# Layer 0 of a four-layer recurrent model: sums over eight neighbours, three additions and a state's four summands are written differently

## The chip, the cores and the metric

The kernel runs on one core of a Trainium2 chip. The metric is the device time of one execution in microseconds. Three runs of the kernel before took 3638.57, 3640.07 and 3646.86 us; the median is 3640.07. A separate, profiled execution took 3631.03 us.

Each core has five engines with queues of their own: TensorE (PE in the profile, its weight loads PEld), VectorE (DVE), ScalarE (ACT), GpSimd (POOL), and SyncE (SP), which here only starts DMA transfers. An engine works through its queue in order; engines wait for each other by semaphores.

## The reference, cut to what matters

The model has four layers; each computes `x + s * silu(g)` from a recurrent or attention branch s and an expert branch g. Only layer 0 is touched. Its branch s is a linear recurrence over time for 16 heads of 8 features, for 8 sequences of 512 tokens of 128 features:

```python
def step(S, inp):
    r_, w_, k_, v_, kk_, b_ = inp
    sab = jnp.einsum('bhvk,bhk->bhv', S, kk_)
    S = S * jnp.exp(w_)[:, :, None, :] + sab[..., None] * b_[:, :, None, :] + v_[..., None] * k_[:, :, None, :]
    y = jnp.einsum('bhvk,bhk->bhv', S, r_)
    return (S, y)
_, y = jax.lax.scan(step, S0, (rh, wh, kh, vh, kkh, bh))
mu = y.mean(-1, keepdims=True)
var = ((y - mu) ** 2).mean(-1, keepdims=True)
yn = (y - mu) / jnp.sqrt(var + 0.00064) * ln_w + ln_b
bonus = (r4 * k4 * time_faaaa).sum(-1, keepdims=True) * v4
out = (yn + bonus).reshape(B, T, C) * g
return out @ output.T
```

The vectors r, w, k, v, kk and b of every token come from the token and the one before it, through a difference xx (previous minus current), small matrix products and activations; kk is divided by its norm over the 8 features of a head. The expert branch picks tokens for each of 48 experts, runs a two-layer network on them and adds the results into an array in DRAM.

## The kernel before, in words

**Stages.** The 512 tokens are cut into four *stages* of 128 (`jt`, `JT` = 4). For each stage there are four pieces of work:

- *Front* (`front`, two halves of four sequences each, `hf`): features on the partitions. xx on Vector (L375), products on TensorE (L377 to L415), activations on ACT, the rest on Vector: L388 (four inputs), L443 and L444 (the sum of squares over 8 features, nrm), L449 to L454, and L455 (yb plus t1), L457, L459. The last writes Kt.
- *Back* (`back`): six arrays are transposed by TensorE (L619) and copied by ACT (L620) so that the 128 pairs of sequence and head lie on the partitions; then Vector prepares pairs of steps: bonus, dk, dr (L628 to L648), each a product and a reduce over 8, with a scratch tile `sg` of one buffer.
- *Scan* (L687 to L720): two tokens are treated in one step, so a stage has 64 steps, in eight *blocks* of eight (`SH` = 8). A block first prepares Z (L687, L691); a step then has five pairs of Vector instructions, one for each half of a state's rows: L700, L704, L706, L710, L712. Z holds for a step four summands of 8 x 8 elements; L710 and L712 add them in two rounds to the new state Hs. After the steps the block multiplies the states by r (L714, L715, L718) into HR and sums over 8 (L720) into Y.
- *Closing* (L721 to L764): a correction of Y (L723), mean and variance over 8 (L727 to L730), scale and offset on ACT (L736), addition of the bonus term (L739), eight transposes on TensorE (L748), the product with the gate (L749), transposes (L754) and the output product (L758).

**Experts.** `experts()` is a generator with 49 *turns*. A turn has one expert's first products (L562), for every second one the gathering of two more experts' tokens (L548, L552), and the former expert's second products (L574), transpose (L582), scaling and scatter (L585). Two turns are taken before each block, so all are done at the start of stage 3.

**What sets the order.** From here on TensorE's order is the order of the program text (`manual_schedule`): for each stage, the front and back of the *next* stage, then the experts' turns with what stands between them, then the closing of this stage. The queues of Vector, ACT and GpSimd are ordered by the framework's scheduler, ahead of time; the order is fixed when the kernel runs. The first stage's front stands earlier, beside the picking of tokens (L493 to L497), which is Vector work.

**Buffers.** `k.pa` is a ring of five PSUM banks for everything but the experts, which have three others. HR and Z have one buffer, Hs two, Y one.

## Time and profile before

| What | Value |
|---|---|
| Median of three runs | 3640.07 us |
| Profiled execution | 3631.03 us |
| Span of its instructions | 3629.3 us |
| Busy over the span: TensorE / Vector / ACT / GpSimd | 2764.3 / 2336.2 / 1642.4 / 745.4 us |
| Mean granted TensorE clock | 0.835 of full speed |
| First scan step (L700), last (L712) | 201.9 us, 856.1 us |
| Scan groups L700, L704, L706, L710, L712 (512 each), busy | 108.8, 87.6, 91.5, 91.6, 82.1 us |
| L720 (32), busy | 38.8 us |

The profile gives, for each group of instructions, the line, engine and operation, the output and input tiles with their shapes, how many there are, their busy time and the mean length of one in ns, and the idle time of the engine before them with what ended it. Busy time counts overlapping instructions once; Vector's short instructions overlap with the one before by some 0.08 us, so that mean lengths add up to more than the busy time. A timeline line has start, length, engine, line, operation and tiles, the count, and in brackets the idle time before it. A product of two 32-bit matrices shows as two records and two weight loads, a transpose as one. A window's line has its length, then busy time and count of each engine, the granted TensorE clock, the DMA share and GB/s.

### The profile page before, as it was taken

How to read it: one execution, taken by the hardware profiler on the slowest of the kernel's cores; microseconds unless marked ns; L12 is line 12 of the kernel's file. 1: busy time of each engine (PE TensorE's matmuls, PEld its weight loads, DVE VectorE, ACT ScalarE, POOL GpSimd, SP SyncE). 2: the span in 40 equal slices, each digit the busy share in tenths (PEclk: the TensorE clock that was granted, in tenths of full speed). 3: DMA queues.
4: the chain of work that ended last, by engine and by line, in shares of the span. 5: the costliest groups of instructions: out<-in, count | busy, mean ns of one | idle time of the engine just before them, and what ended most of it. 6: DMA issues, size and time to landing. Idle time of an engine off the chain costs nothing.

```text
span 3629.3 us, 44988 instructions
## 1 busy us (share of the span) xinstructions
PE 2764.3 (76%) x16390; PEld 1479.4 (41%) x16390; DVE 2336.2 (64%) x6346; ACT 1642.4 (45%) x3207; POOL 745.4 (21%) x845
## 2 busy tenths in 40 slices
PE   6164656512998898799999999998678877778777
PEld 4143444401444454344444444444334444444444
DVE  7989898998583234334445445445478787777776
ACT  5163545512544455233333333333266666655655
POOL 0004050400125553201101101101112222222121
PEclk8585757555789899799899899899878898878989
DMA  4003030311002222100000000000000000000000
GB/s 120 2 2 72 1 81 1 72 49 34 1 2 47 39 42 29 56 1 1 1 1 1 1 1 1 1 1 1 6 15 1 4 4 4 1 3 4 1 4 7
DMA packets 67519, 64.53 MB, mean 18 GB/s; under 512 B 5344, under 2 KB 59616, under 8 KB 66784
## 3 DMA queue, kind: packets, MB, share of 16 engines
q1 hardware_dynamic: 39264, 42.75, 3.8%
q0 software_dynamic: 19712, 14.69, 3.1%
q10 hardware_dynamic: 8320, 4.19, 0.4%
q8 instruction: 129, 2.11, 0.2%
q14 instruction: 94, 0.77, 0.1%
HBM read 43.80 MB, written 17.83 MB: 17 GB/s over the span
## 4 chain that ended last, share of the span: by engine, by line
PE 35%; DVE 16%; ACT 7%; issue 2%; POOL 2%; DMA 0%; POOLq 0%; ACTq 0%; DVEq 0%; SPq 0%
PE pa L1372 6%; PE pu L1390 6%; DVE nm L1972 4%; ACT at L1973 3%; PE pu L1969 3%; PE pf L1954 2%; DVE mpad L1404 2%; PE pf L1435 2%; PE pa L1486 1%; PE pa L1485 1%; ACT at L1422 1%; PE pa L1878 1%; PE pa L1509 1%; PE pa L1359 1%; PE pa L1515 1%
## 5 line engine op out<-in xcount | busy, mean ns | idle before, releaser
L1973 ACT ACTIVATE at<-pu,nm 128x512 f32<-128x512 f32 x512 | 347.9, 688 | 174.3 <-DVE nm L1972 154.5
L1972 DVE TENSOR_REDUCE nm<-pu 128x1 f32<-128x512 f32 x512 | 327.4, 683 | 75.4 <-PE pu L1969 74.8
L199 POOL TENSOR_SCALAR_AFFINE_SELECT at<-at 128x512 f32<-128x512 f32 x184 | 123.6, 672 | 1000.2 <-ACT at L1422 851.7
L1404 DVE TENSOR_REDUCE mpad<-pu 128x2 f32<-128x256 f32 (+3 forms) x256 | 199.2, 819 | 168.1 <-PE pu L1401 168.1
L1422 ACT ACTIVATE at<-pu 128x1024 f32<-128x1024 f32 (+3 forms) x256 | 171.8, 702 | 283.5 <-PE pu L1390 283.2
L1078 ACT ACTIVATE at<-pu,rsqrt 128x1024 f32<-128x1024 f32 (+3 forms) x256 | 191.1, 793 | 191.0 <-PE pu L1073 161.2
L1372 PE MATMUL pa<-hid,f 128*128 128x512 f32 x512 | 222.7, 593 | 0.0
L1969 PE MATMUL pu<-qT,kT 32*128 32x512 f32 x1024 | 203.1, 731 | 2.4 <-ACT at L1973 2.3
L1390 PE MATMUL pu<-qT,kT 32*128 32x512 f32 (+3 forms) x1024 | 160.6, 514 | 56.4 <-DVE mpad L1404 41.8
L748 PE MATMUL pa<-ident,Y 128*128 128x128 f32 x32 | 7.9, 425 | 211.2 <-DVE Y L739 211.2
L1954 PE MATMUL pf<-at,va 128*32 128x512 f32 x1024 | 163.1, 715 | 0.4 <-POOL va L1947 0.4
L1390 PE MATMUL pu<-kT,qT 32*128 32x128 f32 (+3 forms) x1024 | 150.8, 565 | 14.7 <-ACT at L1422 10.5
L548 POOL DMA_INDIRECT xg<-xn_d,idx x48 | 55.1, 1147 | 499.5 <-PE pf L552 318.5
L1372 PEld LDWEIGHTS pa<-hid,f 128*128 128x128 f32 x512 | 96.6, 190 | 119.5 <-issue 118.9
L1493 DVE SCALAR_TENSOR_TENSOR X<-X,u 128x512 f32<-128x512 f32 x56 | 38.7, 691 | 156.7 <-ACT u L1488 156.7
L1073 PE MATMUL pu<-qT,kT 32*128 32x512 f32 (+3 forms) x1024 | 130.3, 513 | 4.9 <-ACT at L1078 3.9
L1016 POOL DMA_INDIRECT f_d<-ys,idx x64 | 105.0, 1640 | 140.0 <-DMA f_d<-ys,idx 85.2
L1947 POOL TENSOR_TENSOR va<-V,sm 128x32 f32<-128x32 f32 x128 | 36.7, 286 | 463.6 <-DVE sm L1946 384.0
L1390 PEld LDWEIGHTS pu<-qT,kT 32*128 32x128 f32 x1024 | 67.3, 196 | 154.4 <-DVE mpad L1404 114.3
L1373 ACT ACTIVATE hid<-pa,f 128x512 f32<-128x512 f32 x64 | 44.0, 688 | 172.5 <-PE pa L1372 172.5
L1083 DVE TENSOR_TENSOR at<-at,ceiling 128x512 f32<-128x512 f32 x72 | 50.0, 695 | 102.3 <-ACT at L1078 91.4
L700 DVE TENSOR_TENSOR Z<-Hs,KE 128x96 f32<-128x96 f32 x510 | 108.8, 253 | 0.9
(610 smaller groups left out, 6682.8 us busy)
## 6 DMA issues: line engine op xcount, KB each, us to landing
w<-in_w_dram SPq DMA_DIRECT2D x24, 512.0 KB, 3.7
f_d<-zeros ACTq DMA_DIRECT2D x8, 512.0 KB
xn_d<-xn SPq DMA_DIRECT2D x8, 512.0 KB, 5.0
w<-in_w_dram SPq DMA_DIRECT2D x16, 256.0 KB, 3.2
w<-in_w_dram SPq DMA_DIRECT2D x24, 128.0 KB
f<-in_f_dram SPq DMA_DIRECT2D x1, 2888.0 KB, 11.9
xn<-in_x_dram SPq DMA_DIRECT2D x4, 512.0 KB, 9.0
Gt<-in_x_dram SPq DMA_DIRECT2D x4, 512.0 KB
```

The costliest lines, as they stand in the source:

```text
L199: self.nc.gpsimd.affine_select(a, a if src is None else src, pattern, ALU.is_ge, 0.0, base=0, channel_multiplier=-1)
L700: nc.vector.tensor_tensor(z[:, 0:3, v, :], bc(prev[:, v, :], 1, 3), bc(KE[:, o + t, 0:3, :], 2, 4), ALU.mult)
L1073: nc.tensor.matmul(pu[:, n, 0:m], q["kT"][r, g // 2, kc * P : kc * P + P], q["qT"][r, g, kc * P :], start=True, stop=True,)
L1078: nc.scalar.activation(at_[:, i : i + 2, 0:m], pu[:, :, 0:m], AF.Square, bias=k.rsqrt2, scale=32.0**-0.5)
L1372: nc.tensor.matmul(ps, fn[n][:, c0 : c0 + P], src[:, i, :], start=(i == 0), stop=(i == 3))
L1390: self.k.nc.tensor.matmul(pu[:, n, 0:m], a[r, c0 : c0 + P], b[r, q0 : q0 + m], start=True, stop=stop)
L1404: nc.vector.tensor_reduce(top[:, i : i + 2, 16], pu[:, :, 0:m], AX.X, ALU.max)
L1422: nc.scalar.activation(at_[:, i : i + 2, 0:m], pu[:, :, 0:m], AF.Exp, scale=8.0**-0.5)
L1954: nc.tensor.matmul(po[i * 32 : i * 32 + 32, :], va[:, kc, c0 : c0 + 32], E[:, i, :], start=(kc == 0), stop=(kc == JT - 1))
L1969: nc.tensor.matmul(pu, q["kT"][r, kc * P : (kc + 1) * P], q["qT"][r, g, :], start=True, stop=True)
L1972: nc.vector.tensor_reduce(nm[:, w], pu, AX.X, ALU.max, negate=True)
L1973: nc.scalar.activation(E[:, n, :], pu, AF.Exp, bias=nm[:, w], accum_out=sm[:, w])
```

## The change

- A helper `eighths` sums over groups of eight neighbours by TensorE: eight products with the identity as the stationary matrix, each with every eighth element as the moving one, accumulate in one PSUM bank. It takes the place of Vector's reduces L443, L630, L638, L640, L720, L727 and L730. Some results are read by Vector or ACT where they lie; bonus, dr and Y are copied to SBUF by ACT.
- Y's sums (`outputs`) are issued one block later, between the two expert turns that stand before the next block; the last block's come after the loop. HR gets two buffers.
- The difference xx is two products, with the identity and with its negative, and a copy by ACT; yb plus t1 is two products; the addition of the bonus term L739 goes into the transposes, which become pairs of products (L772 of the changed kernel).
- In the scan, L710 and L712 become one TENSOR_REDUCE for each half (L735 of the changed kernel), which adds the four summands of a state; its innermost axis has a step of 64 elements.

```diff
--- before.py
+++ after.py
@@ -357,6 +357,16 @@
         flat = lambda a: a.rearrange("p a b -> p (a b)")
         hv = lambda a: a.rearrange("p b (h n) -> p (b h) n", n=8)
         s_v = s.rearrange("p (b j) c -> p b j c", j=JT)
+        minus = cp.tile([P, P], F32, name="minus0")
+        nc.gpsimd.tensor_scalar(minus, k.ident, -1.0, None, ALU.mult)
+
+        def eighths(src):
+
+            ps = k.pa(src.shape[:2])
+            for i in range(8):
+                nc.tensor.matmul(ps, k.ident, src[:, :, i], start=(i == 0), stop=(i == 7))
+            return ps
+
 
         own = cp.tile([P, 4, C], F32, name="own0")
         for i, n in enumerate(("receptance", "key_w", "key_w", "value")):
@@ -371,8 +381,11 @@
                 bs = slice(hf * 4, hf * 4 + 4)
                 cur, prev = xT[:, bs, t0 + 1 : t0 + P + 1], xT[:, bs, t0 : t0 + P]
                 ht = lambda nm, sh=(P, 4, C): hp.tile(list(sh), F32, name=nm)
-                xx = ht("xx")
-                nc.vector.tensor_tensor(xx, prev, cur, ALU.subtract)
+                xx = k.pa((P, 4, C))
+                nc.tensor.matmul(xx, k.ident, prev, start=True, stop=False)
+                nc.tensor.matmul(xx, minus, cur, start=False, stop=True)
+                xs = ht("xx")
+                nc.scalar.copy(xs, xx)
                 ps = k.pa((P, 4, C))
                 nc.tensor.matmul(ps, w1m, cur, start=True, stop=False)
                 nc.tensor.matmul(ps, w1p, prev, start=False, stop=True)
@@ -385,7 +398,7 @@
                     q = slice(f * 32, f * 32 + 32)
                     nc.tensor.matmul(ps, cn["maa_w2"][q, :], mix[q, :, :], start=True, stop=True)
                     t.append(ht(f"xf{f}"))
-                    nc.vector.scalar_tensor_tensor(t[f], ps, cn["maa"][:, f : f + 1], xx, ALU.add, ALU.mult)
+                    nc.vector.scalar_tensor_tensor(t[f], ps, cn["maa"][:, f : f + 1], xs, ALU.add, ALU.mult)
                 trg, twa, tk_, tv_ = t
 
                 def both(ps, w, t):
@@ -440,8 +453,7 @@
                 pn = tokens((cur, own[:, 2]), (tk_, own[:, 2]), (lk, cn["k_w2"][:, 0:C]))
                 nc.scalar.activation(t2, pn, AF.Square)
                 nrm = ht("nrm", (P, 64))
-                nc.vector.tensor_reduce(nrm, hv(t2), AX.X, ALU.add)
-                nc.vector.tensor_scalar(nrm, nrm, 1e-24, None, ALU.max)
+                nc.vector.tensor_scalar(nrm, eighths(hv(t2)), 1e-24, None, ALU.max)
                 nc.scalar.activation(t1, t1, AF.Exp, scale=-1.0)
                 nc.scalar.activation(t1, t1, AF.Ln, bias=1.0)
                 nc.scalar.activation(nrm, nrm, AF.Ln)
@@ -452,9 +464,11 @@
                 nc.vector.scalar_tensor_tensor(a_, a_, 1.0, not_ma, ALU.subtract, ALU.mult)
                 pk = tokens((cur, own[:, 1]), (tk_, own[:, 1]))
                 nc.vector.scalar_tensor_tensor(a_, a_, 1.0, pk, ALU.add, ALU.mult)
-                nc.vector.tensor_tensor(yb, yb, t1, ALU.add)
-                nc.scalar.activation(F["EWt"][:, bs, :], yb, AF.Exp, scale=-1.0, bias=k.less_half)
-                nc.vector.scalar_tensor_tensor(yb, yb, 0.5, mk_, ALU.add, ALU.mult)
+                ps = k.pa((P, 4, C))
+                nc.tensor.matmul(ps, k.ident, yb, start=True, stop=False)
+                nc.tensor.matmul(ps, k.ident, t1, start=False, stop=True)
+                nc.scalar.activation(F["EWt"][:, bs, :], ps, AF.Exp, scale=-1.0, bias=k.less_half)
+                nc.vector.scalar_tensor_tensor(yb, ps, 0.5, mk_, ALU.add, ALU.mult)
                 nc.scalar.activation(t1, yb, AF.Exp, scale=-1.0)
                 nc.vector.tensor_tensor(F["Kt"][:, bs, :], a_, t1, ALU.mult)
 
@@ -627,18 +641,21 @@
             bonus = bp.tile([P, P], F32, name="bonus", bufs=2)
             tt(t, Rs.rearrange("p t s n -> p (t s) n"), BK[:, 1].rearrange("p t s n -> p (t s) n"), ALU.mult)
             tt(t, t, bc(cn["time_faaaa"], 1, P), ALU.mult)
-            nc.vector.tensor_reduce(bonus, t, AX.X, ALU.add)
-            t = work().rearrange("p (a t n) -> p a t n", a=2, n=8)
-            dk = bp.tile([P, 2, HT], F32, name="dk")
+            nc.scalar.copy(bonus, eighths(t))
+            pairs = lambda: work().rearrange("p (a t n) -> p a t n", a=2, n=8)
+            both = lambda t: eighths(t.rearrange("p a t n -> p (a t) n"))
             dr = bp.tile([P, 2, HT], F32, name="dr", bufs=2)
             bk = BK[:, :, :, 0, :]
             kk, kk2, w, w2 = (KE[:, :, i, :] for i in range(4))
             b2, r = BK[:, 0, :, 1, :], Rs[:, :, 0, :]
+            t = pairs()
             tt(t, bk, bc(kk2, 1, 2), ALU.mult)
-            nc.vector.tensor_reduce(dk, t, AX.X, ALU.add)
+            dk = both(t).rearrange("p (a t) -> p a t", a=2)
+            t = pairs()
             tt(t, bk, bc(r, 1, 2), ALU.mult)
-            nc.vector.tensor_reduce(dr, t, AX.X, ALU.add)
+            nc.scalar.copy(dr.rearrange("p a t -> p (a t)"), both(t))
             tt(bk, bk, bc(w2, 1, 2), ALU.mult)
+            t = pairs()
             tt(t, bc(dk, 3, 8), bc(b2, 1, 2), ALU.mult)
             tt(bk, bk, t, ALU.add)
             tt(r, r, w, ALU.mult)
@@ -656,12 +673,18 @@
         carry = cp.tile([P, 8, 8], F32, name="carry0")
         nc.gpsimd.memset(carry, 0.0)
         ready = back(*first)
+
+        def outputs(HR, y):
+
+            nc.scalar.copy(y, eighths(HR.rearrange("p t s v n -> p (t s v) n")))
+
         for jt in range(JT):
             G, KE, BK, Vs, Rs, bonus, kr = ready
             if jt + 1 < JT:
                 ready = back(*front(jt + 1))
             Y = bp.tile([P, P, 8], F32, name="Y")
             yp = Y.rearrange("p (t s) v -> p t s v", s=2)
+            last = None
             for o in range(0, HT, SH):
                 if jt == JT - 1 and o // SH >= HT // SH - JT:
 
@@ -679,8 +702,10 @@
                         nc.vector.tensor_tensor(s_v[:, :, j, :], f, old, ALU.add)
                     else:
                         held = f, old
-                for _ in range(2):
-                    next(side, None)
+                next(side, None)
+                if last:
+                    outputs(*last)
+                next(side, None)
 
                 Z = up.tile([P, SH, 4, 8, 8], F32, name="Z", bufs=1)
                 for i in range(2):
@@ -707,28 +732,27 @@
                             z[:, 0:2, v, :], bc(sab[:, h], 3, 8), bc(BK[:, 0, o + t], 2, 4), ALU.mult
                         )
                     for h, v in halves:
-                        nc.vector.tensor_tensor(z[:, 0:2, v, :], z[:, 0:2, v, :], z[:, 2:4, v, :], ALU.add)
-                    for h, v in halves:
-                        nc.vector.tensor_tensor(Hs[:, t, v, :], z[:, 0, v, :], z[:, 1, v, :], ALU.add)
-                HR = up.tile([P, SH, 2, 8, 8], F32, name="HR", bufs=1)
+                        nc.vector.tensor_reduce(
+                            Hs[:, t, v, :], z[:, :, v, :].rearrange("p s v n -> p v n s"), AX.X, ALU.add
+                        )
+                HR = up.tile([P, SH, 2, 8, 8], F32, name="HR")
                 nc.vector.tensor_tensor(HR[:, 0, 0], carry, bc(Rs[:, o, 0, :], 1, 8), ALU.mult)
                 nc.vector.tensor_tensor(
                     HR[:, 1:, 0], Hs[:, 0 : SH - 1], bc(Rs[:, o + 1 : o + SH, 0, :], 2, 8), ALU.mult
                 )
                 nc.vector.tensor_tensor(HR[:, :, 1], Hs, bc(Rs[:, o : o + SH, 1, :], 2, 8), ALU.mult)
                 carry = Hs[:, SH - 1]
-                nc.vector.tensor_reduce(yp[:, o : o + SH], HR, AX.X, ALU.add)
+                last = HR, Y[:, o * 2 : (o + SH) * 2, :].rearrange("p t v -> p (t v)")
+            outputs(*last)
             t3 = fp.tile([P, B, C], F32, name="EWt").rearrange("p b (h n) -> p (b h) n", n=8)
             nc.vector.tensor_tensor(t3[:, 0:HT], Vs[:, :, 0, :], bc(kr, 2, 8), ALU.mult)
             nc.vector.tensor_tensor(yp[:, :, 0, :], yp[:, :, 0, :], t3[:, 0:HT], ALU.add)
 
 
             mu = bp.tile([P, P], F32, name="mu")
-            nc.vector.tensor_reduce(mu, Y, AX.X, ALU.add)
-            nc.vector.scalar_tensor_tensor(Y, Y, 8.0, bc(mu, 2, 8), ALU.mult, ALU.subtract)
+            nc.vector.scalar_tensor_tensor(Y, Y, 8.0, bc(eighths(Y), 2, 8), ALU.mult, ALU.subtract)
             nc.scalar.activation(t3, Y, AF.Square)
-            nc.vector.tensor_reduce(mu, t3, AX.X, ALU.add)
-            nc.scalar.activation(mu, mu, AF.Ln, bias=k.eps_gn, scale=1.0 / 8)
+            nc.scalar.activation(mu, eighths(t3), AF.Ln, bias=k.eps_gn, scale=1.0 / 8)
             nc.scalar.activation(mu, mu, AF.Exp, scale=-0.5)
             nc.vector.tensor_tensor(t3, Vs.rearrange("p t s n -> p (t s) n"), bc(bonus, 2, 8), ALU.mult)
             nc.vector.tensor_tensor(Y, Y, bc(mu, 2, 8), ALU.mult)
@@ -736,7 +760,6 @@
                 nc.scalar.activation(
                     Y[:, :, n], Y[:, :, n], AF.Identity, scale=cn["ln_w"][:, n : n + 1], bias=cn["ln_b"][:, n : n + 1]
                 )
-            nc.vector.tensor_tensor(Y, Y, t3, ALU.add)
 
             YT = fp.tile([P, B, C], F32, name="Rt")
             oTs = fp.tile([P, B, P], F32, name="Kt")
@@ -745,7 +768,10 @@
             for n0 in range(0, 8, 4):
                 ps = k.pa((P, 4, P))
                 for i in range(4):
-                    nc.tensor.transpose(ps[:, i, :], Y[:, :, n0 + i], k.ident)
+                    for src in (Y, t3):
+                        nc.tensor.matmul(
+                            ps[:, i, :], src[:, :, n0 + i], k.ident, start=(src is Y), stop=(src is t3)
+                        )
                 nc.vector.tensor_tensor(yv[:, n0 : n0 + 4, :], ps, gv[:, n0 : n0 + 4, :], ALU.mult)
             for b0 in range(0, B, 4):
                 oT = oTs[:, b0 : b0 + 4, :]
```

## The prediction

> **What bounds the kernel now.** I read the page's slices first, then the busy time by stage of layer 0, the groups by shape, and the timeline of one block and of one stage boundary. Of the slices, Vector is near full only up to 860 us, which is layer 0:
>
> ```profile
> span 3629.3 us, 44988 instructions
> DVE  7989898998583234334445445445478787777776
> ```
>
> Busy time, the four windows being the four scan stages of 128 tokens (the columns are named in its second line):
>
> ```profile
> core 0: us, PE busy (x) PEld busy (x) DVE busy (x) ACT busy (x) POOL busy (x), PEclk, DMA share, GB/s
> 200.00:362.00 162.00, 94.10 (x567) 68.89 (x566) 149.73 (x736) 81.25 (x164) 41.63 (x30) 0.70 0.19 41
> 362.00:542.00 180.00, 114.93 (x640) 81.19 (x640) 164.26 (x751) 94.95 (x190) 44.10 (x31) 0.68 0.18 41
> 542.00:717.00 175.00, 112.34 (x640) 80.70 (x640) 162.37 (x749) 94.52 (x189) 43.22 (x28) 0.70 0.17 37
> 717.00:857.00 140.00, 9.78 (x59) 7.31 (x59) 137.99 (x711) 20.51 (x32) 6.41 (x4) 0.52 0.14 33
> ```
>
> Vector is busy 614 of 657 us: here its queue is the bound, and TensorE has half its time free. TensorE's largest wait is for the end of a stage:
>
> ```profile
> PE pa L748 <- DVE Y L739: 211.2, 4, 124.2
> ```
>
> So, before, TensorE ran through the next stage's front and back and this stage's experts without looking at the scan, and waited only at the end. Its program order is fixed by hand; that matters below.
>
> **The scan.** One step on Vector, and two ends of blocks:
>
> ```profile
> 334.42 0.43 DVE L700 TENSOR_TENSOR Z<-Hs,KE 128x96 f32<-128x96 f32 x2
> 334.77 0.34 DVE L704 TENSOR_REDUCE sab<-Z 128x8 f32<-128x64 f32 x2
> 335.02 0.35 DVE L706 TENSOR_TENSOR Z<-sab,BK 128x64 f32<-128x64 f32 x2
> 335.29 0.35 DVE L710 TENSOR_TENSOR Z<-Z 128x64 f32<-128x64 f32 x2
> 335.56 0.31 DVE L712 TENSOR_TENSOR Hs<-Z 128x32 f32<-128x32 f32 x2
> 335.79 0.42 DVE L700 TENSOR_TENSOR Z<-Hs,KE 128x96 f32<-128x96 f32 x2
> ...
> 331.80 1.21 DVE L720 TENSOR_REDUCE Y<-HR 128x128 f32<-128x1024 f32 x1
> 347.14 1.21 DVE L720 TENSOR_REDUCE Y<-HR 128x128 f32<-128x1024 f32 x1
> ```
>
> Instructions overlap, so starts count, not durations. A step is 335.79 - 334.42 = 1.37 us: 0.87 for L700 to L706 and 0.50 for the two additions (L710, L712) of both halves. A block of eight steps is 15.34.
>
> *A state's four summands in one sum.* The 0.50 goes; two TENSOR_REDUCE of 128 elements come, call their pitch together x. L704 reads 64 elements at a pitch of 0.125, L720 reads 1024 at 1.13, so a reduce costs 0.058 + 1.047 ns an element: 0.192 for 128, x = 0.38, if it reads as those do. But they read dense rows, and the new one steps 64 elements (256 bytes) from one summand to the next. The Trainium skill (Advanced Engine Details and Errata, section Memory Cachelines) says that SBUF is read in lines of 16 bytes and that a new line at each access is penalised; it gives no figure. The nearest row is L749, whose 32-byte steps, on one input and on the output, take a 128x512 product from the 0.692 of L718 to 1.066: 0.73 ns more an element.
>
> ```profile
> L718 DVE TENSOR_TENSOR HR<-Hs,Rs 128x512 f32<-128x512 f32 x32 | 22.1, 692 | 1.0
> L749 DVE TENSOR_TENSOR Rt<-pa,Gt 128x512 f32<-128x512 f32 x8 | 8.4, 1066 | 1.3 <-PE pa L748 1.3
> ```
>
> With it the reduce is 0.286, x = 0.57. As an outer bound, half rate gives 0.326, x = 0.65. By dense rows the sum saves 0.12 a step, by row and rule it loses 0.07 (0.15). I take 0.57. In L749 the output is stepped too, so it may be the writing alone that is dear; 0.38 stays as the lower end.
>
> *Sums over eight neighbours.* Each becomes eight accumulating products with the identity. Four products of the same form (L562, eight records, as each takes two) took 1.06 us with a warm clock and 1.91 at the lower granted one: 2.1 to 3.8 us for eight, against 1.13 of Vector pitch. Their moving operand steps 32 bytes. Here I do not follow the rule: weight loads with such steps (L619 of Kt, 222 ns) cost what dense ones do (L754, 223 ns). Off Vector go: L720 in each block; per stage the reduces of bonus, dk, dr and of mean and variance (5 x 1.13) and L739 (1.15); per half front xx, nrm and yb+t1 (3 x 0.6). To ACT come 0.37 us copies of the sums and a 0.6 us copy of xx. ACT is half idle; these count only on the path below.
>
> A block becomes 15.34 - 1.13 + 8(x - 0.50): 13.3, **14.8**, 15.4 us for the three x.
>
> **What is moved: a new wait.** A block's products HR now stay until TensorE has summed them, and HR has two buffers. So the third block's products (first row L739 of the new code) wait for the first block's sum. In TensorE's order that sum stands behind the whole front and back of the *next* stage and three expert turns. The scheduler's order of the new kernel shows the same: in stages 0 to 2 all of the next front's second half and back stand on Vector's queue ahead of the third block's HR rows, and 58 of the fourth block's 64 scan instructions behind them. Before, these were strewn among scan steps. While Vector waits there, nothing of the scan can pass. I follow stage 1 by its times in the trace of before:
>
> ```profile
> 389.88 0.55 PEld L377 LDWEIGHTS pa<-xT,w1m 128*128 128x128 f32 x2
> 455.44 0.68 DVE L459 TENSOR_TENSOR Kt<-sg,t 128x512 f32<-128x512 f32 x1
> 464.67 0.50 PE L562 MATMUL pf<-xgT,w 128*128 128x128 f32 x3
> 479.41 0.33 PE L582 MATMUL pf<-ident,yT 128*128 128x128 f32 x1 [0.81 <-ACT yT L578]
> 541.56 1.21 DVE L720 TENSOR_REDUCE Y<-HR 128x128 f32<-128x1024 f32 x1
> ```
>
> These are the next front's first product, its Kt, the first and third expert turn, and the stage's end (its HR rows end at 541.5).
>
> 1. Closing of the stage before: Vector's new order holds, from the last HR row to the second closing product, 64 + 5 scan instructions of 0.18, 3.1 of closing additions and products ahead of these, two set-ups and HR rows: 24.0 us, plus 3.2 of waiting for eight-product sums of 3.8 that 2 us of steps don't cover. That is 27.2 against 21.0 (361.8 to 382.8): **+6**.
> 2. Front: xx by TensorE in front of the first product, nrm's sum (eight products of 64 columns, 1.3) ahead of pk's products, then yb+t1 (1.0) and xx (1.0) ahead of the second half's first product. That puts its first products 6 us back, of which 3.3 vanish in a time when Vector still had the first half's tail; 1.6 more come at its end. **+4.4**: Kt ends at 460.5 instead of 456.1.
> 3. Back: Kt to the start of L637 took 10.7 (transposes, ACT's twelve copies); then product 1.15, sum 1.9, product 1.15, sum 1.9, since the scratch has one buffer: 16.8.
> 4. Three expert turns: 464.67 to 479.6 is 14.9, less 2.9 in which ACT still had copies of the back: 12.
> 5. The first block's sum and its hand-over: 2.5.
>
> The third block's products so start at 456.1 + 4.4 + 16.8 + 12 + 2.5 + 6 = 497.8. Vector has by then done all the scan it may (from 382.8 it holds some 62 us of work). Left are: HR rows 1.33, 58/64 of eight steps (10.4), HR rows 1.33, four blocks (59.1): 72.2. End 570.0 against 541.5, **+28.5**. Stage 2 has the same order: +28.5. Stage 0 has no closing before it, and its front starts while blocks run: Kt at 258.5 + 4.5 for two half-chains, + 16.8 + 12 + 2.5 = 294.3, + 72.2 = 366.5 against 361.8: **+4.7**. Stage 3 has no next front: 8(14.8 - 15.34) = -4.3, closing rows -3.4, waits in the closing before it +4: **-3.7**. After the last block all is bare: three sums of 3.8 with 0.3 to 0.9 of hand-over and copy for 1.25 each, less 2.5 for L739: **+6.6**.
>
> Sum 4.7 + 57 - 3.7 + 6.6 = 64.6, or 3631 to 3696 against the profiled execution (3631.03, of which 1.7 lies outside the span). The runs' median is 9 above that execution; the sum is of differences, so it goes on 3640.07: **3705 us**. With x = 0.38: -2.7 + 2 x 20.1 - 15.9 + 6.6 = 28, **3668**. With 0.65: 80, 3720.
>
> **The rivals.**
>
> *The stepped read costs nothing* (x = 0.38): 3668. For it: TensorE's weight loads don't mind steps. Against: L749 and the skill's rule. Chance 0.28.
>
> *No wait for HR: Vector's relief is had in full.* The other side. It holds if TensorE gets to the first block's sum before Vector has done its third block; then stages 0 to 2 each lose the front's 3.6, the back's 3.4, the closing's 3.4 and eight blocks' difference (4.3 or 16.5): -15 or -27, and the sum is -45 or -93: 3595 or 3547. It begins to win once the sum comes some 21 us earlier than my 497.8, at about 477, which is before the back alone is through. Against it is TensorE's written order; for it, that my path has waits taken from a time when Vector was crowded. Chance 0.10.
>
> *TensorE becomes the bound.* Per block two expert turns (4.1 each in the steady stretch) and a sum: 10.3 to 12.0, under 14.8. Were stepped moving reads at half rate, 12.4 to 15.8: the blocks would be set by it, and six sums on each stage's path would add 2 to 4 us each, some 40 in all: 3745. Chance 0.08.
>
> **How the numbers follow.** My case (0.54) is 3705, alone 3685 to 3730. The rivals pull the range down to 3650, between the dense reduce and no wait, and up to 3745: at most 2 in 10 lie outside. Within 0.2% (3632.8 to 3647.4) is what a measurement of this kernel can tell from no change. Slower: my case, the dense reduce and TensorE, 0.90 less 0.06 for a path half as long. Faster 0.11, same 0.05, slower 0.84.
>
> **What would show it.** Right: the third block's first HR row in stages 0 to 2 has tens of us of idle before it and behind the front's and back's rows, released by TensorE; the one in stage 3 has none; the new reduce lasts about 0.37 us (0.28 if dense). TensorE's wait at the stage's end (211 us) shrinks and turns into waits for HR. Wrong: Vector still above 90% busy in stages 1 and 2, or stages 1 and 2 no longer than 180 and 175 us.

## The result

The changed kernel takes 3731.37 us (median of four runs, 3728.99 to 3734.13), the one before 3639.32 (four runs, 3637.55 to 3646.86): a ratio of 1.025, interval 1.0236 to 1.0264, or **92 us slower**. The forecast was 3705, with a range of 3650 to 3745. The profiled executions differ by 99.7 us in span (3729.0 and 3629.3); the accounts below are made on these.

The span and Vector's slices, on the page of the kernel after:

```profile
span 3729.0 us, 46703 instructions
...
DVE  7877759399457333533454444444467787767776
```

Up to the tenth slice Vector was 7 to 9 tenths busy before; now it falls to 5 and 3 tenths in two slices of the scan (the sixth and the eighth). By stage, in windows cut at the ends of the last HR rows (columns as in the windows of before):

```profile
208.00:382.70 174.70, 136.80 (x782) 107.59 (x782) 141.48 (x594) 79.24 (x171) 41.63 (x30) 0.84 0.17 38
382.70:594.60 211.90, 162.15 (x920) 130.29 (x920) 149.70 (x602) 93.54 (x198) 44.54 (x32) 0.84 0.16 35
594.60:810.00 215.40, 163.68 (x920) 131.01 (x920) 149.68 (x602) 93.54 (x198) 41.09 (x29) 0.83 0.15 31
810.00:946.40 136.40, 54.77 (x242) 49.54 (x242) 129.32 (x573) 22.24 (x39) 3.10 (x2) 0.61 0.13 32
```

Vector's busy time did fall, from 163 and 162 us to 150 in stages 1 and 2; but it is now busy 150 of 212 us instead of 163 of 179. TensorE rose from 115 and 112 to 162 and 164. The following table has the start of the first stage, the lengths of the four stages, each from the end of its predecessor's last HR rows to the end of its own, and what is left of the span after them (closing and the other layers), for these two kernels and those of the experiments.

| Kernel | start | stage 0 | 1 | 2 | 3 | rest |
|---|---|---|---|---|---|---|
| before | 201.8 | 160.2 | 179.1 | 175.2 | 140.8 | 2772 |
| after | 208.2 | 174.4 | 211.9 | 215.4 | 136.4 | 2783 |
| after, turns later | 201.5 | 167.0 | 208.8 | 211.4 | 134.8 | 2764 |
| after, front and back spread | 208.0 | 166.0 | 207.9 | 215.0 | 145.2 | 2787 |
| after, Y's sums on Vector | 202.9 | 161.8 | 173.2 | 186.4 | 164.0 | 2771 |
| the same, fewer turns a stage | 202.7 | 161.8 | 173.2 | 189.8 | 154.4 | 2777 |
| before with Y's sums by TensorE | 201.7 | 157.5 | 194.9 | 197.1 | 135.0 | 2769 |
| before with the front's part | 205.5 | 153.4 | 174.2 | 180.5 | 142.3 | 2768 |

The stages changed by +14.2, +32.8, +40.2 and -4.4; the start by +6.4, the rest by +10.3. (The rest moves between 2764 and 2787 among kernels that are alike in the other layers, so little is read from it.) Where stage 1's time goes is seen in the timeline of after; these lines answer to the five of stage 1 shown in the prediction (closing's second product, the next front's first product, its Kt, the back's products, the first block's sum, the third block's HR rows):

```profile
410.38 1.07 DVE L775 TENSOR_TENSOR Rt<-pa,Gt 128x512 f32<-128x512 f32 x1 [1.84 <-PE pa L772]
417.89 1.06 PE L385 MATMUL pa<-xT,ident 128*128 128x512 f32 x1
483.56 0.69 DVE L473 TENSOR_TENSOR Kt<-sg,t 128x512 f32<-128x512 f32 x1 [0.69 <-ACT t L472]
489.15 1.23 DVE L642 TENSOR_TENSOR sg<-Rs,BK 128x1024 f32<-128x1024 f32 x1 [4.89 <-ACT Rs L634]
496.76 1.22 DVE L652 TENSOR_TENSOR sg<-BK,KE 128x1024 f32<-128x1024 f32 x1 [4.52 <-PE pa L367]
502.07 1.23 DVE L655 TENSOR_TENSOR sg<-BK,Rs 128x1024 f32<-128x1024 f32 x1 [3.36 <-PE pa L367]
516.75 3.90 PE L367 MATMUL pa<-HR,ident 128*128 128x128 f32 x16
520.69 0.22 DVE L739 TENSOR_TENSOR HR<-Hs,Rs 128x64 f32<-128x64 f32 x1 [9.26 <-PE pa L367]
```

The third block's HR rows start 138.0 us after the stage before ended (520.7 less 382.7), released by the first block's sum; from there Vector needs 73.9 us to the stage's end. Of Vector's waits (the wait's owner, its releaser, us in total, times, longest) the two largest new ones are these, and below them TensorE's largest for the scan:

```profile
DVE nrm L456 <- PE pa L367: 61.9, 8, 20.3
DVE HR L739 <- PE pa L367: 31.5, 7, 9.3
```

```profile
PE pa L367 <- DVE HR L743: 95.7, 12, 12.6
```

Before, TensorE waited 211 us for the closings' Y. Of these 124 fall to stage 3, where it had nothing else to do; the rest is the time that it had to spare in stages 0 to 2, ahead of the transposes of each closing:

```profile
379.23 1.97 PE L748 MATMUL pa<-ident,Y 128*128 128x128 f32 x8 [47.46 <-DVE Y L739]
558.34 1.97 PE L748 MATMUL pa<-ident,Y 128*128 128x128 f32 x8 [23.36 <-DVE Y L739]
733.54 1.97 PE L748 MATMUL pa<-ident,Y 128*128 128x128 f32 x8 [16.20 <-DVE Y L739]
```

In the changed kernel what is left at these places is 7.6 us ahead of a stage's last HR sum, and 1.1, 2.5 and 4.0 inside its closing.

Vector had run out of work well before it stood at the HR rows: in stage 1 it waited 19.0 us at nrm of the second half, and then at each product of the back.

### The profile page after: what moved, and what is told of

Its sections match the earlier page's. It is cut to its first block, busy times and chain, and to the rows that moved or that the text cites. A ratio compares the mean times of both kernels' runs of the same rounds, so it can differ in the third digit from the quotient of the medians.

```text
span 3729.0 us, 46703 instructions
## 1 busy us (share of the span) xinstructions
PE 3002.4 (81%) x17510; PEld 1701.5 (46%) x17510; DVE 2273.7 (61%) x5754; ACT 1636.6 (44%) x3240; POOL 737.6 (20%) x846
## 5 line engine op out<-in xcount | busy, mean ns | idle before, releaser
L367 PE MATMUL pa<-HR,ident 128*128 128x128 f32 x512 | 126.4, 415 | 95.7 <-DVE HR L743 95.7
L735 DVE TENSOR_REDUCE Hs<-Z 128x32 f32<-128x128 f32 x512 | 164.8, 362 | 0.0
L367 PEld LDWEIGHTS pa<-HR,ident 128*128 128x128 f32 x512 | 114.5, 270 | 103.1 <-issue 71.1
```

Of the source, the lines that this page charges most:

```text
L367: nc.tensor.matmul(ps, k.ident, src[:, :, i], start=(i == 0), stop=(i == 7))
L735: nc.vector.tensor_reduce(Hs[:, t, v, :], z[:, :, v, :].rearrange("p s v n -> p v n s"), AX.X, ALU.add)
```

## The experiments

All ratios are to the kernel before on the same chip. Every kernel here computes the reference.

**1. The four-summand reduce alone.** The kernel before, with this edit:

```diff
-                        nc.vector.tensor_tensor(z[:, 0:2, v, :], z[:, 0:2, v, :], z[:, 2:4, v, :], ALU.add)
-                    for h, v in halves:
-                        nc.vector.tensor_tensor(Hs[:, t, v, :], z[:, 0, v, :], z[:, 1, v, :], ALU.add)
+                        nc.vector.tensor_reduce(
+                            Hs[:, t, v, :], z[:, :, v, :].rearrange("p s v n -> p v n s"), AX.X, ALU.add
+                        )
```

> The kernel before with one edit: the two additions of a scan step become the one reduce over four summands. Theory (the stepped read is dear): the reduce's pitch is 0.28 us as in the changed kernel (0.56 for both halves instead of 0.50), 256 steps x 0.06 = 15 us, and as Vector sets the pace here, 3639 + 15 = 3654. If the reduce were dense in price (0.38 for both halves): 3639 - 31 = 3608. If the scan did not set the pace: 3639.

Measured: 0.9995 (0.9988 to 1.0002), no difference. The reduce itself is as dear as forecast; its group in this run:

```profile
L710 DVE TENSOR_REDUCE Hs<-Z 128x32 f32<-128x128 f32 x512 | 165.4, 362 | 0.0
```

A block of nothing but scan takes 15.62 us against 15.34, so 0.28 more, where 0.56 was expected. Blocks that share Vector with a front or back came out shorter, and the stages as wholes differ from before by -0.4, -2.5, -1.3 and +1.1. That the scheduler has two instructions fewer to place in each step may be why; it was not tested.

**2. The two additions put back into the changed kernel.** The same edit the other way round.

> The changed kernel with the two additions put back. Theory (the scan waits for HR in stages 0 to 2): only what comes after the wait gets faster, 4.9 blocks of 0.48 us in each of three stages (7), plus 3.8 in stage 3, plus 1 in the closings: 3731 - 12 = 3719. If Vector's own work set the pace everywhere: 3731 - 15 = 3716, hardly to be told apart; if the reduce were the main cause of the loss, 3731 - 92 = 3639.

Measured: 1.0269 (1.0247 to 1.0292) against 1.025 with the reduce. No gain: the reduce is not where the 92 us are.

**3. What a dense reduce of that size costs.** The kernel before, with 512 more reduces:

```diff
+                    for h, v in halves:
+                        nc.vector.tensor_reduce(
+                            spare[:, h], z[:, :, v, :].rearrange("p s v (m n) -> p s (v m) n", n=4), AX.X, ALU.add
+                        )
```

> The kernel before, with one more reduce for each half of each step: 128 elements read as dense rows of 4, into a scratch tile that nobody reads, so the result is the same and 512 Vector instructions come on top. If a reduce costs by its elements alone, as L704 and L720 say, one is 0.28 us long and the time rises by 512 x 0.19 = 98 us, to about 3727. If dense and stepped reads cost the same (0.36 long, pitch 0.28), it is some 143 us, about 3772; then the step of 256 bytes isn't what makes the new reduce long.

Measured: 1.0279 (1.026 to 1.0299), some 102 us, or 109 in span. The group of the added reduces:

```profile
L711 DVE TENSOR_REDUCE spare<-Z 128x32 f32<-128x128 f32 x512 | 121.0, 276 | 0.0
```

Equal in size, 276 ns dense and 362 with steps of 256 bytes: the step costs 86 ns, 0.67 an element, and with dense reads the sum of four would be cheaper than two additions: the 102 us are 0.40 a step, against 0.50.

**4. The first block's sum no longer behind expert turns.** The changed kernel, its sums ahead of a block's turns, and no turns before the first two:

```diff
-                next(side, None)
                 if last:
                     outputs(*last)
-                next(side, None)
+                for _ in range((0, 0, 3, 3, 3, 3, 2, 2)[o // SH]):
+                    next(side, None)
```

> The changed kernel with the expert turns of each stage moved: none before the first two blocks, then 3, 3, 3, 3, 2, 2, so that the first block's sum follows the back at once. Theory: the third block's products start 12 us earlier in stages 0 to 2, at best 3731 - 36 = 3695; three turns and a sum (14.4 to 16.1 us) then pace the next four blocks against 14.6 by Vector, which gives back up to 6 us a stage: 3695 to 3713. If the expert turns are not in the way of the sum: 3731.

Measured: 1.0189 (1.0169 to 1.0208), some 22 us less than after, as many as the first expectation had, but not where it had them. Stages 1 and 2 lose only 3 to 4 us each, where the prediction had 12 us of turns on the path; stage 0 loses 7. Of the 42 us between the two profiles, 26 are in the start and after stage 3, outside of the edited loop. In stage 1 the third block's rows start 133.6 us after the stage before. These are TensorE's longest waits between the closing and the end of stage 1:

```profile
PE pf L596 <- ACT yT L592: 18.4, 15, 2.3
PE pa L633 <- DVE Kt L473: 3.0, 1, 3.0
PE pa L406 <- DVE xf L401: 2.3, 2, 1.9
```

There is no wait for the scan among them, nor among the shorter ones. From the end of one closing to the stage's end TensorE is busy or in hand-overs of the front, the back and the experts, and Vector's wait at the third block's HR rows is down to 2.5 us. A second limit stands a few us behind the first.

**5. The next front and back cut in three and spread over the stage**, in the changed kernel, so that no HR sum stands behind all of them:

```diff
-            if jt + 1 < JT:
-                ready = back(*front(jt + 1))
...
                     outputs(*last)
+                if jt + 1 < JT:
+                    if o == SH:
+                        made = front(jt + 1, 0)
+                    elif o == 3 * SH:
+                        front(jt + 1, 1, made)
+                    elif o == 5 * SH:
+                        ready = back(*made)
```

> The changed kernel, but the next stage's front and back no longer stand in one piece ahead of all of TensorE's work of a stage: the front's first half comes after the second block's sum is issued, its second half in the fourth block, the back in the sixth. No HR sum then stands behind more than one of these. If only the place of the sums in TensorE's order costs (my theory as predicted), stages 1 and 2 take some 180 us and the time is 3630 to 3650 with the kernel before at 3630. If TensorE's own work in order (closing 28, front and back 75, sixteen turns 70, eight sums of 2 to 4 each, some 200 us in all) is what is too long for a stage, it comes to 3670 to 3700.

Measured: 1.0241 (1.0226 to 1.0257), as the changed kernel; above both expectations. Stages 1 and 2 take 207.9 and 215.0. TensorE's longest waits in stage 1, which again has none for the scan:

```profile
PE pf L599 <- ACT yT L595: 24.7, 13, 5.7
PE pa L367 <- DVE sg L658: 1.4, 1, 1.4
```

So the order alone is not to blame: what TensorE has to do in one stage takes some 208 to 215 us with its hand-overs, with the front and back in one piece or spread. That agrees with what it had to spare: it is busy for 162 and 169 us of stages 1 and 2 here, 47 and 57 more than before, against waits of 23 and 16 before. That is 23 and 41 too much, and the stages are 29 and 40 longer than before. Vector is busy for 150 of them.

**6. Y's sums back on Vector**, all else as changed (HR again with one buffer):

```diff
-                if last:
-                    outputs(*last)
...
-                last = HR, Y[:, o * 2 : (o + SH) * 2, :].rearrange("p t v -> p (t v)")
-            outputs(*last)
+                nc.vector.tensor_reduce(yp[:, o : o + SH], HR, AX.X, ALU.add)
```

> The changed kernel with the sum over HR on Vector again, as before (one HR buffer, no sums of Y on TensorE); all else as changed. Theory (the wait for HR is the cause): the wait is gone and with it most of the loss. Vector per stage loses 10.4 us of front, back and closing and gains 3.9 by the reduce; but TensorE's own chain was only 7 us shorter than Vector's in the stage before (closing 28, front and back 75, sixteen turns 70 of 180 us) and is now some 12 us longer, so stages 0 to 2 come out near +5 us each, the start +6, the end +3: about 3639 + 20 = 3660. If TensorE's chain has slack: 3639 - 10 = 3629. If the loss comes from the other sums (fronts, backs, closings) and not from HR: near 3731.

Measured: 1.0099 (1.0078 to 1.0121), which takes away some 55 of the 92 us. Stage 0 takes 1.6 more than before, stage 1 even 5.9 less; the loss is in stages 2 and 3. The closing of stage 2, whose Y was ready at 727.2, shows it:

```profile
754.22 2.05 PE L367 MATMUL pa<-Y,ident 128*128 128x128 f32 x8
758.21 1.22 DVE L750 SCALAR_TENSOR_TENSOR Y<-Y,pa 128x1024 f32<-128x1024 f32 x1 [22.68 <-PE pa L367]
```

The mean is now a sum on TensorE, behind expert turns that end only at 754: Vector waits 22.7 us. In stage 1, too, the turns end 23 us after Vector's last HR rows (560.7 against 537.9): even without HR's sums TensorE's work is longer than a stage.

**7. Besides that, fewer turns a stage**: fourteen in each of stages 0 to 2, eight in stage 3. **8. The same in the kernel before.**

```diff
+                for _ in range(1 if jt < JT - 1 and o // SH >= HT // SH - 2 else 2):
+                    next(side, None)
```

> The changed kernel with Y's sums on Vector again (as in the run that took this part out) and, besides, fourteen expert turns in each of stages 0 to 2 and the last eight in the first four blocks of stage 3, where TensorE has nothing to do. With sixteen turns a stage that kernel stood 30 us above the one before, and its trace showed the loss at the end: the closing of stage 2 began some 27 us late on TensorE, behind the last turns. If TensorE's work in order is what fills a stage, this loss goes: 3615 to 3635 with the kernel before at 3630. If the rest of the loss is in the waits that nrm's, dk's and dr's sums put into Vector's queue, it stays at 3650 to 3660.

Measured: 1.0055 (1.0042 to 1.0069). That is 3650 at 3630 before, the number of the second expectation, but not its cause: nrm's waits are 2.7 us in stage 2, and those for the back's sums come to 5.6. Vector's longest waits in stages 2 and 3 are still the closings' means, the one of stage 1 being

```profile
556.59 1.22 DVE L750 SCALAR_TENSOR_TENSOR Y<-Y,pa 128x1024 f32<-128x1024 f32 x1 [13.65 <-PE pa L367]
```

and that of stage 2 9.6 us; they make up most of what these stages are longer than before (14.6 and 13.6). The last turn's transpose of stage 1 starts 14.6 us after Vector's last HR rows end (552.3 against 537.7). So the first expectation had the cause, and two turns fewer were not enough of a cut. Against number 6, stage 3 became 10 us shorter and stage 2 3 longer; the two were not measured on one chip.

> The kernel before with fourteen expert turns in each of stages 0 to 2 and the last eight in stage 3. Vector's queue sets the pace there and TensorE ends a stage some 7 us ahead of it, so relief of TensorE alone gives little: 3622 to 3632, no change by 2%. If TensorE's order already set the ends of stages, stages 1 and 2 lose up to 8 us each: 3610 to 3618. If the late scatters hold up the loads of stage 3, it is slower, 3640 or more.

Measured: 1.0036 (1.0023 to 1.0049), slower. Stages 0 to 2 are unchanged (159.8, 178.8, 175.4), so TensorE did not set their length before; stage 3 grew from 140.8 to 151.4, where a Vector instruction waits 11.2 us for a loaded piece of the experts' result, as the third expectation had it.

**9 to 12. Each part alone, in the kernel before**: the front's (xx, nrm, yb plus t1), the back's (bonus, dk, dr), the closing's (mean, variance, bonus term), and Y's sums with the second HR buffer. The edits are those parts of the change's diff.

> The kernel before with only the front's part of the change: xx and yb plus t1 as products, nrm's sum by eight products. Vector is relieved of 3.6 us a stage; TensorE gets some 9 more in a stage in which it ended 7 ahead of Vector. If Vector's busy time decides, -14 us; if TensorE's work in order decides, 0 to +10.

Measured: **0.9966** (0.9956 to 0.9976), 12 us faster, and so faster than either kernel. The first expectation comes near; the second, that TensorE had only 7 us to spare, fails. Where the 12 us are is not shown: the profiled execution is 10 us above the median, and its stages and start together are 1 us shorter than before.

> The kernel before with only the back's part: the sums for bonus, dk and dr by eight products each. Vector is relieved of 3.4 us a stage. By my step 3 the back takes 16.8 us on TensorE's path in place of nothing that TensorE waited for, less the 7 that it had to spare: +10 a stage in stages 1 and 2, some +15 to +25 in all. If only Vector's busy time counts, -10 to -14.

Measured: 1.0014 (1.0005 to 1.0023), 5 us slower; neither expectation. The four stages together are 1 us shorter than before, and the first starts 5.8 later. My step 3 alone does not lengthen the stages: TensorE still waits 14 us for the closing at the ends of stages 1 and 2.

> The kernel before with only the closing's part: mean and variance summed by TensorE, the bonus term added in the transposes. By my steps 1 and the one for the end: two sums and hand-overs of 10 us on the bare path after the last block, less what Vector drops, +4; 4 to 8 more at each of the three other closings if TensorE's work in order decides: +10 to +25. If these lie hidden behind scan steps, +2 to +5.

Measured: 1.0000 (0.9992 to 1.0009). After the last HR rows the closing is 7.9 us longer up to its last product (34.4 against 26.5), but stages 1 and 2 are 2.9 and 1.8 shorter.

> The kernel before with only Y's sums by TensorE, one block later, and two HR buffers; the two additions of a state stay. Taking this part out of the changed kernel gained 55 us. If TensorE's work in order decides, a stage of it comes to the 173 us of before and eight sums of 3.9, some 204 in stages 1 and 2 (179 and 175 before): +50 to +60 in all. If only the wait of the third block counts, with front and back as short as before, it starts some 122 us after the stage and has 74 left: stages of 196, +35 to +40. If the parts are dear only together, under +20.

Measured: 1.0077 (1.0052 to 1.0103), 28 us slower. Stages 1 and 2 take 194.9 and 197.1, the 196 of the second expectation; stages 0 and 3 gain 2.7 and 5.8, which it had left out, so that the whole falls between its +35 and the third expectation's 20. The first sum and the rows that wait for it, in stage 1 of this run:

```profile
475.89 3.92 PE L367 MATMUL pa<-HR,ident 128*128 128x128 f32 x16
...
479.85 0.23 DVE L732 TENSOR_TENSOR HR<-Hs,Rs 128x64 f32<-128x64 f32 x1 [6.08 <-PE pa L367]
```

That is 120.7 us after the stage before (359.2), and 74.3 before the end: the same path as in the changed kernel, 17 us shorter. Here it is the wait alone that sets the stage, for TensorE has time left at its end; it waits for the closing's Y:

```profile
573.21 1.12 PE L767 MATMUL pa<-ident,Y 128*128 128x128 f32 x4 [14.96 <-DVE Y L758]
```

**The parts do not add up.** Alone, the five come to -0.05, -0.34, +0.14, 0 and +0.77%: +0.52%, some 19 us. Together they cost 92. The missing 73 us are what the parts cost each other. In the kernel before, TensorE's longer fronts, backs and closings lie in time that it has to spare. The front's part alone shows this. In the kernel before, the last expert transpose of stage 1 came ahead of the end of the HR rows (541.0), and TensorE then waited 23.4 us for the closing, as shown above:

```profile
534.50 0.48 PE L582 MATMUL pf<-ident,yT 128*128 128x128 f32 x1 [1.23 <-ACT yT L578]
```

With the front's part the same transpose comes after that end (533.0), and still TensorE waits 13.3 us:

```profile
538.05 0.48 PE L596 MATMUL pf<-ident,yT 128*128 128x128 f32 x1 [2.76 <-ACT yT L592]
...
551.78 1.97 PE L762 MATMUL pa<-ident,Y 128*128 128x128 f32 x8 [13.25 <-DVE Y L753]
```

All parts together want more than there is to spare. And once the HR sums stand behind fronts, backs and closings in TensorE's order, each us of these is a us of the path: from Y's sums alone to all parts, the third block's rows go from 120.7 to 138.0 us in stage 1 and from 121.8 to 143.1 in stage 2. Of the 73.9 us between the profiles of these two kernels, 52 lie in stages 0 to 2 and 1 in stage 3; 6.5 in the start and 13.6 after stage 3 are not explained by this path.

## Why the prediction was right, and where it was off

**The mechanism held.** The third block's HR rows wait for the first block's sum, in stages 0 to 2, and the sum stands behind the next front and back and three turns. Number 12, with Y's sums alone, shows the same path. In stage 1 its terms against the trace, from the end of one stage:

| Step | forecast | measured |
|---|---|---|
| 1. closing, to its second product | 27.2 | 27.7 |
| 2. front, from there to Kt's end | 77.7 | 73.9 |
| 3. back, to the first turn | 16.8 | 23.0 |
| 4. three turns | 12 | 9.5 |
| 5. first sum and hand-over | 2.5 | 3.9 |
| third block's HR rows | 136.2 | 138.0 |
| from there to the stage's end | 72.2 | 73.9 |

The single terms miss by -3.8 to +6.2 us and cancel to 1.8, so that the sum is this close is in part luck. Stage 1 grew by 32.8 where 28.5 were forecast, and stage 3 changed by -4.4 where -3.7 were. (The forecast took 541.5 for the end of stage 1's HR rows before; they end at 541.0, so its addition should read 29.)

In part of its signs the prediction was too plain: the idle ahead of the HR rows themselves is 9.3 us at most, since Vector had stood still already at nrm and at the back's products. Stage 3's third block waits too, but only 1.8 us; it was to have no wait.

**Where 35 us of the profile were missed** (64.6 forecast, 99.7 measured; 27 by the medians): 16.0 in stage 0, 4.3 in stage 1, 11.7 in stage 2, 3.7 in the rest, less 0.7 in stage 3. Stage 2 was given stage 1's 28.5 and took 40.2. Of these 11.7, 4.3 are stage 1's own miss again, and 3.9 are that I gave both the same addition, where both come to about the same length and stage 2 had been the shorter one (175.2 against 179.1). Another 5.1 are that its third block starts later than stage 1's (143.1 against 138.0), while 1.6 less follow behind it. The front is why. These windows hold TensorE's work of the next front in stages 1 and 2, the granted TensorE clock being the third number from the end:

```profile
417.90:480.70 62.80, 58.59 (x321) 39.05 (x320) 32.83 (x120) 36.41 (x53) 0.00 (x0) 0.98 0.00 1
629.40:698.40 69.00, 63.89 (x322) 43.67 (x320) 34.78 (x124) 36.41 (x53) 0.00 (x0) 0.90 0.00 1
```

The same front takes 62.8 us at a clock of 0.98 and 69.0 at 0.90. I had reckoned both at one speed. In number 2, with the same work on TensorE, it is the other way round: to the end of Kt the front took 70.2 us in stage 1 at a clock of 0.93 and 66.5 in stage 2 at 0.98, and the third block's rows started 142.8 and 139.2 us after the stage before. On this path through TensorE the clock counts.

Stage 0 was forecast at +4.7, counted from the Kt of before (258.5) and 4.5 us more for the front. What this left out is that TensorE's order has the first stage's back, with its three new sums, ahead of the next front. That front's first product came right behind the transposes before, and comes behind the last sum now, 19.8 us later. Before:

```profile
183.24 1.13 PE L377 MATMUL pa<-xT,w1m 128*128 128x512 f32 x2 [0.16 <-ACT KE L620]
```

After:

```profile
199.11 4.08 PE L367 MATMUL pa<-sg,ident 128*128 128x128 f32 x16 [1.41 <-DVE sg L655]
203.01 1.89 PE L385 MATMUL pa<-xT,ident 128*128 128x512 f32 x2
```

The front itself, at a clock of 0.91, was 3 us shorter than before, so that Kt ended at 275.1 where 263.0 were forecast; the back took 6.3 us more than its step, the turns 5.2 less. Stage 0's end is 20.7 later, 16 more than forecast.

A part of this is the later start, +6.4, of which the forecast had none: the first front stands on Vector's queue among the picking of tokens, and there its nrm and yb wait (3.1, 2.8, 4.6 and 3.3 us in the four places, against 1.9 and 4.9 before). How much is lost there is not fixed by these sums: numbers 4, 6 and 7 have the same first front and start at 201.5 to 202.9, and in number 4 the waits at nrm and yb come to 7.5 us in place of 13.8.

After the stages, +10.3 against +6.6; of it the closing, up to the last addition, has 8.5 (36.4 against 27.9).

**TensorE's sums.** The step on the cost of eight products took 1.9 to 3.8 us and set the rule on new lines aside for TensorE, since weight loads didn't mind steps. The sums of 128 columns took 3.9 to 4.1 everywhere. This is where the back's 6 us come from: two sums at 1.9, and the one for bonus reckoned like Vector's reduce of before. These two groups stand a few us apart in the trace of after, eight records of dense expert products and sixteen of a sum:

```profile
524.07 1.06 PE L576 MATMUL pf<-xgT,w 128*128 128x128 f32 x8
...
527.41 3.90 PE L367 MATMUL pa<-HR,ident 128*128 128x128 f32 x16
```

A record of 128 columns takes 0.13 us there and 0.24 here, and the windows of the first and the two halves of the second show that it isn't the clock, for the second half, at half the clock, is no slower than the first:

```profile
524.10:525.10 1.00, 1.00 (x11) 1.00 (x10) 1.00 (x8) 0.37 (x1) 0.00 (x0) 1.00 0.49 139
...
527.50:529.30 1.80, 1.80 (x10) 1.61 (x9) 1.80 (x11) 0.37 (x1) 1.50 (x2) 1.00 0.80 182
529.30:531.20 1.90, 1.90 (x10) 1.90 (x9) 1.90 (x11) 0.00 (x0) 1.33 (x2) 0.52 0.19 50
```

Nor is it the accumulation: the accumulated dense products for yb and t1 (L468, L469) take 1.02 us for two records of 512 columns each, the same 0.13 for 128. So at the full clock a moving operand with steps of 32 bytes reads at about half rate, as the Trainium skill has it in general (Advanced Engine Details and Errata, section Memory Cachelines: a new 16-byte line at each access is penalised). At the lower clock little of it is seen (4.11 against 3.78 us), for a dense record then takes nearly as long. Here are sixteen dense records and sixteen of a sum, with windows inside each, both at 0.50:

```profile
299.25 3.78 PE L576 MATMUL pf<-xgT,w 128*128 128x128 f32 x16 [0.46 <-ACT xgT L568]
606.34 4.11 PE L367 MATMUL pa<-EWt,ident 128*128 128x128 f32 x16 [2.46 <-ACT EWt L754]
...
606.40:610.40 4.00, 4.00 (x16) 3.72 (x16) 2.56 (x15) 1.19 (x1) 0.00 (x0) 0.50 0.00 2
299.30:303.00 3.70, 3.70 (x17) 3.70 (x18) 2.94 (x4) 2.34 (x5) 2.10 (x2) 0.50 0.14 38
```

The two rows of weight loads that I went by (222 and 223 ns) were both taken at this lower clock, and so could not show what happens at the full one. Where the path is forecast with the price of a warm clock, as in steps 3 and 5, the rule should have been followed.

**The reduce.** Its 0.57 us a step was right (0.56), its effect wasn't: in the terms for the blocks it came to about +0.07 a step, yet alone it changed nothing. The rival with dense reads is ruled out by numbers 1 and 3. That L749's 0.73 ns an element came so near to the 0.67 of number 3 is no proof of that row: it reads PSUM and writes with steps besides.

**The rivals.** That Vector's relief is had in full was given too much. I had looked for the wait alone, and left out how little TensorE had to spare in stages 1 and 2, 23 and 16 us, against the 47 and 51 that it got. (The 7 us of several expectations are the lead of its last turn over the last HR rows, which is 30, 6 and -1 us in stages 0 to 2; before, TensorE was needed only at the closing's transposes, 17 us later.) Numbers 4 and 5 show what taking the wait away gives: TensorE's 208 us a stage. That rival's -45 or -93 were not to be had by a better order alone, only with less work on TensorE. The rival in which TensorE becomes the bound had its premise right, half rate; it looked at a block, where two turns and a sum are 10.3 us against Vector's 14.6, and there it does not decide. Over a stage it lies only 4 us below the wait. Its 3745 is even nearer to the measured 3731 than my 3705; but in the changed kernel the wait comes last, as the HR rows' 6.5 to 9.3 us show.

**What stays open.** Why the blocks beside fronts and backs got shorter with the reduce; and what number 6 would give with still fewer turns a stage. More HR buffers, which might have taken the wait away without a new order, were not tried.

## What to carry to other kernels

Before work goes from a full engine to a half idle one, add up the idle one's work in its own order between the points where it meets the other, hand-overs included: it is the wait that is left there, here 23 and 16 us in stages of 179 and 175, and not the share of idle time, that can be spent. Each of these moves alone cost little or gained, and together they cost five times their sum, because together they took more than that, and one of them made the others' time count: a result handed back inside the loop, behind long work for later, puts that work on the path. To move it ahead in the order gains little where the engine has no time left (numbers 4 and 5). And parts of a change are to be measured one by one, where the best (the front's part, 0.9966) can be kept.

## What was not expected of the hardware

TensorE's moving operand with steps of 32 bytes takes 0.24 us for a 128x128 record, at a granted clock of 1.00 and of 0.52 alike, where a dense one takes 0.13 at 1.00 and 0.24 at 0.50: the steps cost half the rate at the full clock and little at the lower one. A Vector reduce of 128 elements takes 362 ns with steps of 256 bytes and 276 dense. And a front of the same instructions took 62.8 or 69.0 us, by a granted clock of 0.98 or 0.90.
